# One fused kernel on one core: a one-column Exp behind each Gelu batch, layer 0 in order k, q, v, own rings for passed-on images, three PSUM buffers for the experts' first layer

## The chip, the cores and the metric

The kernel runs on one core of one Trainium2 chip. The metric is the device time of one execution in microseconds (us), as the median of several runs. The engines are named as the profile names them: PE (TensorE, matmuls; PEld its weight loads), ACT (ScalarE), DVE (VectorE), POOL (GpSimd) and SP (SyncE, which here only issues DMAs). SBUF is the on-chip memory with 128 partitions, PSUM the memory that PE writes, in eight banks of 512 float32 columns.

## What is computed

Four residual layers on x of shape (8, 384, 32, 32), all in float32, each layer of the form x + f(groupnorm(x)). Cut to what matters here:

```python
# layer 0: depthwise 3x3, batch norm, Gelu, 1x1 projection for q, k and v; attention; projection; batch norm
y = gelu(bn(depthwise3x3(x)))                 # for each of q, k, v, with own weights
q, k, v = (einsum('oc,bchw->bohw', pw, y) for ...)   # 8 heads of 48
attn = softmax(einsum('bhcn,bhcm->bhnm', q, k) * 48 ** -0.5)
out = bn(einsum('oc,bchw->bohw', w_out, einsum('bhnm,bhcm->bhcn', attn, v)))
# layer 1: 4 experts of one hidden layer (384 -> 384 -> 384, relu), weighted by a top-2 gate
hdn = relu(einsum('bchw,edc->ebdhw', x, w1) + b1)
out = einsum('ebohw,ebhw->bohw', einsum('ebdhw,eod->ebohw', hdn, w2) + b2, coef)
# layer 2: depthwise 7x7 with reflected edges, plus bias
# layer 3: three branches of depthwise convolutions (1, 3, 5) and small MLPs, fused by a gate, projected
```

## The kernel before

An image is N = 1024 pixels, the 384 channels are NC = 3 tiles of 128 partitions, there are B = 8 images. The program runs in stages, told apart in the profile by their lines: layer 0's depthwise convolution (to about 277 us), attention (to about 1745 us), the experts of layer 1 (to about 2705 us), then layers 2 and 3.

The order of instructions on PE, ACT and DVE is the order of the program text (`tc.manual_schedule`); in layer 0's convolution and from the experts on, POOL's too. The order on SP is the planner's. Each engine works in its own order and waits on semaphores for others. A tile pool gives each `tag` a ring of `bufs` buffers; a new tile of a tag waits until the readers of the tile that had its buffer are done. With `reuse_waits="tile"` dependencies are kept by tile.

**Layer 0 (L431 to L538).** `groups` runs over channel tile ct, over v = 0, 1, 2 (q, k, v) and over u = 0..3, a quarter of the output; m = n // 4 numbers the nine (ct, v) pairs. One step is 96 matmuls into one of two four-bank PSUM tiles, then `evict_slots` copies the tile to `o` on ACT (L365). While pair m runs, DVE handles pair m - 1 in `results` (L458): per image a transpose, two `bn_stats` and a store to `raw[v][b]` in DRAM. When the last channel tile of q or k has been handled, `coefs0` turns its statistics into the scale and shift of the batch norm. For image 0, q and k are loaded back to `ys0` and put through Gelu by `gelu0` while v is being convolved: all of q before the eviction of step u = 1, all of k before that of step u = 3 (L531 and L533). After the loop come the eight `results` of v and its `coefs0`.

**Attention (L561 to L913).** For each image: Gelu of q (`activate(b, 0)`), `project_k`, Gelu of v, `project_q`, then sixteen steps of scores and values. The Gelu of k for image b + 1 is done in the middle of image b (L873). At image 0 q and k come from `ys0`, and v's Gelu stands between the second and third tile of `project_q` (L843). `project` and `scores` take two-bank PSUM tiles from a ring of three (`two_banks`, L620). `scores` fills one tile by PE for each of four m and empties it by an Exp on ACT (L736). Gelu and Exp need different activation tables, and a table load (ACT_TABLE_LOAD) is placed by the compiler before an ACTIVATE whose table isn't loaded. `spread` (L634) moves q and k from PSUM to their tiles with an affine on ACT and copies on DVE (for k of image 0 all on ACT). At the end (L877 to L913) the last output projection collects three PSUM results `outs`; ACT copies each to `z`, and DVE takes moments from each. From these follow the coefficients of the next norm (`middle`, L919).

**Experts (L1087 to L1331).** For each image b and half h: twelve hidden tiles `ph` of three logical matmuls each (L1302), each emptied by a Relu on ACT into `hs` (L1306); DVE adds pairs of hidden tiles (`sums`), after k = 9 for the first three experts and at the end for the fourth; then fifteen `products` (L1213) that DVE adds to the residual `r`. In h = 1 `logits` computes the gate of the image (PSUM tiles `pl` and `pt`). In h = 0 of the next image the steps of `next_layer` stand between the Relus, at k = 0, 2, 3, 4, 5, 6: moments, group sums (`gn_ps`), coefficients and then `pass_on` for ct = 0, 1, 2. `pass_on` (L991) norms a channel tile on ACT into `xn2`, transposes it on DVE into `x2`, lets POOL copy the reflected edges and has SP store it to `x2mem` (L999). For the last image `pass_on` comes with the first matmuls of layer 2, and its first tile goes to layer 2's input directly.

Of the kernel before, what the change touches and what calls it, by code (L numbers as in the profile page):

```python
# [136 lines left out]
def conv_mixer_kernel(ctx: ExitStack, tc: tile.TileContext, a: dict, out: bass.AP):  # L137
# [11 lines left out]
    mhalf = const.tile([P, 24], FP, name="mhalf")  # L149
    nc.gpsimd.memset(mhalf, -0.5)  # L150

    one = const.tile([P, 1], FP, name="one")
    nc.gpsimd.memset(one, 1.0)
    parity = const.tile([P, 2], FP, name="parity")
# [158 lines left out]
    def affine(o, i, s, t, func=AF.Identity):  # L313
        nc.scalar.activation(o, i, func, bias=t, scale=s)  # L314
# [45 lines left out]
    def evict_slots(o, ps, at):  # L360
# [3 lines left out]
        ps = ps.rearrange("p (i e) c b h -> p (b h) i (e c)", i=2)  # L364
        nc.scalar.copy(o, ps)  # L365

    ORDERED = {mybir.EngineType.PE, mybir.EngineType.Activation, mybir.EngineType.DVE}
    ys0 = {}
    pre_pool, cxb_pool = ExitStack(), ExitStack()
    cxb = cxb_pool.enter_context(tc.tile_pool(name="cxb", bufs=1, side="right"))  # L370
    with (
# [38 lines left out]
        with tc.tile_pool(name="cps", bufs=2, space=PSUM, reuse_waits="tile") as cps:  # L410
# [17 lines left out]
                    xt0s[ct][:, :, b, 1 : 1 + H].rearrange("p c h -> p h c"), img(xn)  # L428
                )

            groups = [(ct, v, u) for ct in range(NC) for v in range(3) for u in range(4)]  # L431
            weights0 = {}

            def weights_of(n):
# [26 lines left out]
                bn_stats_of(stats[:, v * NC + ct, 2 * b : 2 * b + 2, :], y)  # L461
                nc.sync.dma_start(out=raw[v][b][:, ct, :], in_=y)

            def gelu0(v):

                for ct in range(NC):
                    i, y = v * NC + ct, ys0[v][:, ct, :]
                    affine(y, y, bn_s[:, i : i + 1], bn_t[:, i : i + 1], AF.Gelu)

            def coefs0(v):  # L470
                i = slice(v * NC, (v + 1) * NC)
# [9 lines left out]
            for n, (ct, v, u) in enumerate(groups):  # L481
                if u == 0:

                    o = co.tile([P, B, H, 32], FP, tag="o", name="o")
                w = weights0.pop(n).rearrange("p r t w -> p r (t w)")
                ps = cps.tile([P, 4, 2, B, H], FP, tag="ps", name="ps")
                for cc in range(2):
                    for k in range(3):
                        for e, d, i in product(range(2), repeat=3):
                            r = slice(64 * i, 64 * i + 64)  # L490
                            nc.tensor.matmul(  # L491
                                ps[64 * d : 64 * d + 64, 2 * i + e, cc],
                                lhsT=w[r, 12 * cc + 6 * e + 3 * d + k, :],
                                rhs=xt0s[ct][r, 16 * d + 4 * u + 2 * e + cc, :, k : k + H],
                                start=k == 0, stop=k == 2,
                            )
                spread0(n + 2)
                weights_of(n + 3)
                m = n // 4
                if n < 2:  # L500
                    for b in range(4 * n, 4 * n + 4):
                        stats2(b)
                if n == 1:
                    norm = gn_steps((mvx[:, 0], mvx[:, 1]), slot0)
                    nc.gpsimd.dma_start(out=xstmem, in_=xst)
                    nc.vector.tensor_copy(gmx, next(norm))
                if n == 2:
                    norms[1] = norms[2] = next(norm)
                for b in {3: (0, 1), 4: (2, 3), 8: (4, 5), 9: (6,), 10: (7,)}.get(n, ()):
                    prepare0(1, b)  # L510
                if m in (3, 4, 5) and u < 2:
                    for b in ((0, 1), (2,), (3, 4), (5,), (6, 7), ())[2 * (m - 3) + u]:
                        prepare0(2, b)
                if (m, u) == (5, 3):
                    cxb_pool.close()
                    pp0 = pre_pool.enter_context(
                        tc.tile_pool(name="pre0", bufs=1, side="right", reuse_waits="tile")
                    )
                    pw = pp0.tile([P, 2, NC, NC, P], FP, tag="pw", name="pw")
                    for i, k in enumerate("qk"):  # L520
                        nc.sync.dma_start(out=pw[:, i], in_=a[f"pw_{k}"])
                if m > 0:
                    for b in ((0,), (1, 2), (3, 4), (5, 6, 7))[u]:
                        results(*last, b, last_o)
                if ct == NC - 1 and v > 0 and u == 1:
                    y0 = pp0.tile([P, NC, N], FP, tag=f"y{v - 1}", name="y0")
                    nc.sync.dma_start(out=y0, in_=raw[v - 1][0])
                    ys0[v - 1] = y0
                if ct == NC - 1 and v > 0 and u == 3:
                    coefs0(v - 1)  # L530
                if m == 8 and u in (1, 3):  # L531
                    gelu0(u // 2)
                evict_slots(o, ps, u)  # L533
                if u == 3:
                    last, last_o = (ct, v), o
            for b in range(B):
                results(*last, b, last_o)
            coefs0(2)  # L538


    zraw = [dram.tile([P, NC, N], FP, tag=f"z{b}", name=f"z{b}") for b in range(B)]
# [9 lines left out]
    def layers(again, early, xst, pre_pool, pp0, pw):  # L551
# [9 lines left out]
        def attention(shifted):  # L561
# [3 lines left out]
            with tc.tile_pool(name="aw", reuse_waits="tile", bufs=1) as aw, tc.tile_pool(  # L565
# [45 lines left out]
                        nc.sync.dma_start(out=y, in_=raw[v][b])  # L611
                        ys[b].append(y)

                def activate(b, v):
                    for ct in range(NC):
                        i = v * NC + ct
                        y = ys[b][v][:, ct, :]
                        affine(y, y, bn_s[:, i : i + 1], bn_t[:, i : i + 1], AF.Gelu)

                def two_banks():  # L620
                    return scp.tile([P, 2, HF], FP, tag="sc", name="sc")
# [212 lines left out]
                for i, t in enumerate(todo):  # L834
                    b, j = t[0], i % per_b
                    if j == 0:
                        begun = b == 0 and not shifted
                        if not begun:
                            activate(b, 0)
                        project_k(b)  # L840
                        if not begun:
                            activate(b, 2)
                        project_q(b, (lambda: activate(0, 2)) if begun else None)  # L843
                        if shifted:
                            shift(b)
                    complete = None
# [23 lines left out]
                        project_out(b - 1, 1)  # L870
                    if j == per_b // 2 + 3:
                        if b + 1 < B:
                            activate(b + 1, 1)  # L873
                        project_out(b, 0)


# [7 lines left out]
                        for oc in ocs:  # L884
                            project_tile(outs[oc], att3 if t == NC else att[:, t, :], oc, t, w_last)

                outs = two_banks()
                outs = [outs[:, 0, :], outs[:, 1, :]]
                project_tiles((NC, 0), range(2))
                av_last = attend(*last, keep=True)  # L890
                outs.append(two_banks()[:, 0, :])
# [98 lines left out]

        def pass_on(r, b, ct, s, t, pool):  # L991

            xn2 = pool.tile([P, 32 * HP], FP, tag="xn2", name="xn2")[:, :N]
            affine(xn2, r[:, ct, :], s[:, ct : ct + 1], t[:, ct : ct + 1])
            if ct == 0 and b == B - 1 and xts:
                return transpose_in(xts[0][:, b], xn2)
            x = pool.tile([P, 32 * HP], FP, tag="xn2", name="x2")
            transpose_in(x.rearrange("p (c h) -> p c h", h=HP), xn2)
            nc.sync.dma_start(out=x2mem[b][ct], in_=x)  # L999

# [86 lines left out]
        def experts():  # L1087
# [166 lines left out]
            def next_layer(b):  # L1254
# [7 lines left out]
                for i, (cts, co) in enumerate(zip(parts, cos)):  # L1262
# [1 line left out]
                        keep_residual(r, b)  # L1264
                    moments2(r, b, cts, mv, dq)
                    yield
                    ps = eh.tile([P, NC, 2, 1], FP, tag=("sm", "pl")[i], name="gn_ps")
                    over_groups(ps, dq, co)
                    yield
                    norm2(ps, b, co, st)  # L1270
# [3 lines left out]
                        yield  # L1274

            def logits(b):
                pl = eh.tile([P, QF], FP, tag="pl", name="pl")
                for ct in range(NC):
                    for g in range(4):
                        nc.tensor.matmul(  # L1280
# [15 lines left out]
            for b, h in product(range(B), range(2)):  # L1296
                hs = ew.tile([P, NC, E, HF], FP, tag="hs", name="hs")
                gating = logits(b)
                for k, (e, dc) in enumerate(TODO):
                    ph = eh.tile([P, HF], FP, tag="h", name="ph", bufs=2)  # L1300
                    for ct in range(NC):
                        nc.tensor.matmul(  # L1302
                            ph, lhsT=w1[:, e, ct, dc * P : (dc + 1) * P], rhs=xns[b, h][:, ct, :],
# [1078 lines left out]
```

## Time and profile before

| What | us |
|---|---|
| median of 3 runs (lowest, highest) | 3211.94 (3209.06, 3213.28) |
| the profiled execution | 3207.34 |
| its span, from first to last instruction | 3205.5 |
| PE busy | 3030.8 |
| DVE busy | 1692.7 |
| ACT busy | 1186.8 |
| POOL busy | 262.7 |
| PE busy in 40 to 277 (of 237.0) | 202.1 |
| PE busy in 277 to 340 (of 63.0) | 52.5 |
| PE busy in 1716 to 1760 (of 44.0) | 30.7 |
| PE busy in 2560 to 3205 (of 645.0) | 575.2 |

"Busy" is the time in which an engine works on an instruction; time in which it only waits is not in it. A window view gives the same for a stretch of time. A wait view names who waited, for whom, how long in total, how often and how long at most. A timeline line gives start, duration, engine, line, operation, what is written and read, and in brackets the idle time of the engine before it with what ended it. What ended a wait is inferred, and where the engine named had long been done, it was another.

### The profile page before, as it was taken

The numbers are of one execution on the slowest core, as the hardware profiler recorded it, in microseconds if no ns is written. First come the engines' busy times: TensorE is split into PE (matmuls) and PEld (weight loads), VectorE is DVE, ScalarE is ACT, GpSimd is POOL, SyncE is SP. The second block draws the span as 40 slices with busy tenths as digits, with TensorE's granted clock in tenths as the row PEclk, the third lists the DMA queues.
The fourth block names the chain that finished last, engine by engine and source line by source line (L and its number), as shares of the span: only waits on it lengthen the run. The fifth ranks groups of instructions, "written<-read, shape, count | busy, mean of one in ns | idle before, by whom it ended". The sixth has DMA issues, their size and how long they took to land.

```text
span 3205.5 us, 42222 instructions
## 1 busy us (share of the span) xinstructions
PE 3030.8 (95%) x17740; PEld 1601.8 (50%) x17740; DVE 1692.7 (53%) x2570; ACT 1186.8 (37%) x1341; POOL 262.7 (8%) x415
## 2 busy tenths in 40 slices
PE   4988999999999999999998999999999999886999
PEld 3774334343433334343433566566566666655543
DVE  6998344444444444444445464564554554457174
ACT  3654453535444353535442221211212212446520
POOL 2432000000000000000001100000000000111400
PEclk9999999999999999999998999999999999988999
DMA  6787111011101111011004021121121113876765
GB/s 220 273 282 268 39 42 62 23 62 42 59 25 59 42 42 62 23 62 43 10 25 161 21 63 40 63 63 40 63 63 40 50 44 109 325 238 227 240 226 187
DMA packets 89089, 322.84 MB, mean 101 GB/s; under 512 B 13608, under 2 KB 16000, under 8 KB 84664
## 3 DMA queue, kind: packets, MB, share of 16 engines
q1 hardware_dynamic: 64936, 251.71, 23.0%
q10 hardware_dynamic: 13776, 35.82, 3.6%
q0 software_dynamic: 10176, 32.51, 3.0%
q8 instruction: 141, 2.31, 0.3%
q14 instruction: 60, 0.49, 0.0%
HBM read 211.66 MB, written 111.68 MB: 101 GB/s over the span
## 4 chain that ended last, share of the span: by engine, by line
PE 74%; DVE 13%; DMA 6%; issue 4%; ACT 2%; POOL 1%; SPq 0%; ACTq 0%; DVEq 0%; POOLq 0%
PE av L748 14%; PE sc L729 14%; PE p L1213 11%; PE ph L1302 11%; PE sc L627 7%; PE sc L682 4%; PE sc L804 4%; DVE stats L212 3%; DVE y L460 2%; DVE hs_sum L1206 2%; DMA x<-x 1%; PE ps L1779 1%; PE po L2193 1%; PE po L2196 1%; PE po L2204 1%
## 5 line engine op out<-in xcount | busy, mean ns | idle before, releaser
L736 ACT ACTIVATE e<-sc 128x1024 f32<-128x1024 f32 x512 | 483.1, 1029 | 544.3 <-PE sc L729 544.0
L1302 PE MATMUL ph<-xn,w 128*128 128x512 f32 x1152 | 506.3, 596 | 11.2 <-ACT hs L1306 8.2
L729 PE MATMUL sc<-qT,kT 64*128 64x512 f32 x2048 | 477.6, 603 | 10.4 <-ACT e L736 10.4
L748 PE MATMUL av<-e,vT 128*64 128x512 f32 x2048 | 467.7, 598 | 0.0
L1306 ACT ACTIVATE hs<-ph,b 128x512 f32<-128x512 f32 x192 | 131.2, 687 | 706.0 <-PE ph L1302 705.6
L1302 PEld LDWEIGHTS ph<-xn,w 128*128 128x128 f32 x1152 | 217.2, 191 | 276.0 <-issue 255.9
L729 PEld LDWEIGHTS sc<-qT,kT 64*128 64x128 f32 x2048 | 185.7, 186 | 297.4 <-issue 228.9
L748 PEld LDWEIGHTS av<-e,vT 128*64 128x64 f32 x2048 | 135.5, 136 | 316.4 <-issue 316.4
L627 PE MATMUL sc<-y,pw 128*128 128x512 f32 x576 | 251.8, 598 | 5.2 <-ACT y L314 5.2
L491 PE MATMUL ps<-xt,wx 64*64 64x256 f32 x3456 | 199.0, 389 | 38.5 <-DVE xt L427 20.1
L764 DVE LOAD_MASK_SELECT sm<-av x64 | 0.9, 14 | 424.1 <-PE av L748 424.1
L1227 DVE TENSOR_TENSOR r<-r,p 128x256 f32<-128x256 f32 x416 | 157.2, 417 | 126.9 <-PE p L1213 126.1
L766 DVE RECIPROCAL inv<-sm 128x512 f32<-128x512 f32 x64 | 214.6, 3353 | 2.2
L491 PEld LDWEIGHTS ps<-xt,wx 64*64 64x64 f32 x3456 | 157.6, 138 | 78.9 <-issue 34.0
L627 PEld LDWEIGHTS sc<-y,pw 128*128 128x128 f32 x576 | 109.7, 192 | 146.9 <-issue 138.4
L1061 PE MATMUL ps<-xt,wx 64*64 64x256 f32 (+1 forms) x2912 | 158.1, 375 | 22.4 <-ACT wx L1535 13.2
L1213 PE MATMUL p<-hs_sum,wsum 128*128 128x256 f32 x768 | 173.6, 379 | 0.0
L1213 PEld LDWEIGHTS p<-hs_sum,wsum 128*128 128x128 f32 x768 | 145.9, 190 | 19.8
L1206 DVE TENSOR_TENSOR hs_sum<-hs,hs_sum 128x768 f32<-128x768 f32 (+1 forms) x192 | 147.0, 780 | 4.9
L1061 PEld LDWEIGHTS ps<-xt,wx 64*64 64x64 f32 x2912 | 111.0, 138 | 67.8 <-ACT wx L1535 15.5
L365 ACT COPY o<-ps 128x2048 f32<-128x2048 f32 x56 | 103.9, 1856 | 79.0 <-PE ps L491 48.2
L682 PE MATMUL sc<-pw_v,y 128*128 128x384 f32 x384 | 127.8, 493 | 5.3 <-ACT y L314 5.3
(319 smaller groups left out, 3250.9 us busy)
## 6 DMA issues: line engine op xcount, KB each, us to landing
raw<-y SPq DMA_DIRECT2D x72, 512.0 KB
y<-raw SPq DMA_DIRECT2D x24, 1536.0 KB
x<-x SPq DMA_DIRECT2D x23, 608.0 KB
xt<-x SPq DMA_DIRECT2D x23, 608.0 KB
w<-in_w ACTq DMA_DIRECT2D x36, 384.0 KB
xn<-in_x SPq DMA_DIRECT2D x24, 512.0 KB
x<-in_x SPq DMA_DIRECT2D x16, 768.0 KB
z<-z POOLq DMA_DIRECT2D x16, 768.0 KB, 4.3
```

The source lines that it names most:

```text
L491: nc.tensor.matmul(ps[64 * d : 64 * d + 64, 2 * i + e, cc], lhsT=w[r, 12 * cc + 6 * e + 3 * d + k, :], rhs=xt0s[ct][r, 16 * d + 4 * u + 2 ...
L627: nc.tensor.matmul(ps[:, h, :], lhsT=w[:, ct, pair, :], rhs=y[:, ct, h * HF : (h + 1) * HF], start=ct == 0, stop=ct == NC - 1,)
L682: nc.tensor.matmul(ps[:, m, :C], lhsT=y[:, ct, (m0 + m) * P : (m0 + m + 1) * P], rhs=pw_v[:, ct, :], start=ct == 0, stop=ct == NC - 1,)
L729: nc.tensor.matmul(sc[:, s, :], lhsT=kTs[b][r, pair, m * P : (m + 1) * P], rhs=qTs[b][r, pair, h * HF : (h + 1) * HF], start=True, stop=True,)
L736: nc.scalar.activation(e, sc, AF.Exp, scale=1.0 if shifted else HD**-0.5)
L748: nc.tensor.matmul(av[64 * s : 64 * s + 64, :], lhsT=vTs[0][:, m, c0 : c0 + 64], rhs=e[:, s, :], start=m == 0, stop=m == N // P - 1,)
L766: nc.vector.reciprocal(inv, sm)
L1061: nc.tensor.matmul(ps[64 * d : 64 * d + 64, 2 * i + e, c % 2, images], lhsT=w[r, d * K7 + k, :], rhs=by_slot(xts[ct])[r, 16 * d + column(c ...
L1206: nc.vector.tensor_add(rows_of(o, hs, s), rows_of(i, hs, s), rows_of(j, hs, s))
L1213: nc.tensor.matmul(ps[:, :QF], lhsT=block(w)[:, e], rhs=rows_of(x, hs, e), start=e == 0, stop=e == E - 1,)
L1227: nc.vector.tensor_tensor(out=o, in0=o, in1=ps[:, :QF], op=op)
L1302: nc.tensor.matmul(ph, lhsT=w1[:, e, ct, dc * P : (dc + 1) * P], rhs=xns[b, h][:, ct, :], start=ct == 0, stop=ct == NC - 1,)
```

## The change

Five edits:

- `activate` gets a flag: with it a one-column Exp into the tile `warm` follows the three Gelus. It is set for v of every image and for k of image b + 1.
- Layer 0 works in the order k, q, v (`VORDER`). The Gelus of k for image 0 come one at a time behind the evictions of u = 0, 1, 2 of v's last channel tile, those of q behind the last eviction.
- The last projection's first two results get a two-bank tile each, and not one between them.
- `pass_on` has a ring of one for `xn2` and a ring of two for `x2`, and not one ring of two for both.
- In the experts' PSUM pool `pl` and the last image's second `gn_ps` share the tag `sm`, and `ph` has three buffers and not two.

```diff
+    warm = const.tile([P, 1], FP, name="warm")
...
+    VORDER = (1, 0, 2)
...
-            groups = [(ct, v, u) for ct in range(NC) for v in range(3) for u in range(4)]
+            groups = [(ct, v, u) for ct in range(NC) for v in VORDER for u in range(4)]
...
-            def gelu0(v):
-
-                for ct in range(NC):
-                    i, y = v * NC + ct, ys0[v][:, ct, :]
-                    affine(y, y, bn_s[:, i : i + 1], bn_t[:, i : i + 1], AF.Gelu)
+            def gelu0(v, ct):
+                i, y = v * NC + ct, ys0[v][:, ct, :]
+                affine(y, y, bn_s[:, i : i + 1], bn_t[:, i : i + 1], AF.Gelu)
...
-                if ct == NC - 1 and v > 0 and u == 1:
-                    y0 = pp0.tile([P, NC, N], FP, tag=f"y{v - 1}", name="y0")
-                    nc.sync.dma_start(out=y0, in_=raw[v - 1][0])
-                    ys0[v - 1] = y0
-                if ct == NC - 1 and v > 0 and u == 3:
-                    coefs0(v - 1)
-                if m == 8 and u in (1, 3):
-                    gelu0(u // 2)
+                before = VORDER[m % 3 - 1]
+                if ct == NC - 1 and m % 3 and u == 1:
+                    y0 = pp0.tile([P, NC, N], FP, tag=f"y{before}", name="y0")
+                    nc.sync.dma_start(out=y0, in_=raw[before][0])
+                    ys0[before] = y0
+                if ct == NC - 1 and m % 3 and u == 3:
+                    coefs0(before)
                 evict_slots(o, ps, u)
+                if m == 8 and u < 3:
+                    gelu0(VORDER[0], u)
                 if u == 3:
                     last, last_o = (ct, v), o
+            for c in range(NC):
+                gelu0(VORDER[1], c)
             for b in range(B):
                 results(*last, b, last_o)
-            coefs0(2)
+            coefs0(VORDER[2])
...
-                def activate(b, v):
+                def activate(b, v, exp=False):
                     for ct in range(NC):
                         i = v * NC + ct
                         y = ys[b][v][:, ct, :]
                         affine(y, y, bn_s[:, i : i + 1], bn_t[:, i : i + 1], AF.Gelu)
+                    if exp:
+                        nc.scalar.activation(warm, one, AF.Exp)
...
                         if not begun:
-                            activate(b, 2)
-                        project_q(b, (lambda: activate(0, 2)) if begun else None)
+                            activate(b, 2, True)
+                        project_q(b, (lambda: activate(0, 2, True)) if begun else None)
...
                         if b + 1 < B:
-                            activate(b + 1, 1)
+                            activate(b + 1, 1, True)
                         project_out(b, 0)
...
-                outs = two_banks()
-                outs = [outs[:, 0, :], outs[:, 1, :]]
+                outs = [two_banks()[:, 0, :] for _ in range(2)]
...
-            xn2 = pool.tile([P, 32 * HP], FP, tag="xn2", name="xn2")[:, :N]
+            xn2 = pool.tile([P, N], FP, tag="xn2", name="xn2", bufs=1)
...
-            x = pool.tile([P, 32 * HP], FP, tag="xn2", name="x2")
+            x = pool.tile([P, 32 * HP], FP, tag="x2", name="x2", bufs=2)
...
-                    ps = eh.tile([P, NC, 2, 1], FP, tag=("sm", "pl")[i], name="gn_ps")
+                    ps = eh.tile([P, NC, 2, 1], FP, tag="sm", name="gn_ps")
...
-                pl = eh.tile([P, QF], FP, tag="pl", name="pl")
+                pl = eh.tile([P, QF], FP, tag="sm", name="pl")
...
-                    ph = eh.tile([P, HF], FP, tag="h", name="ph", bufs=2)
+                    ph = eh.tile([P, HF], FP, tag="h", name="ph", bufs=3)
```

## The prediction

> **What bounds the kernel now.** I read five views in this order: the page's busy table, the windows by stage, the waits on TensorE, the timeline around each kind of wait, and last the table of groups for durations. The page:
>
> ```profile
> PE 3030.8 (95%) x17740; PEld 1601.8 (50%) x17740; DVE 1692.7 (53%) x2570; ACT 1186.8 (37%) x1341; POOL 262.7 (8%) x415
> ```
>
> TensorE is the bound, so only its idle time (about 175 us of 3205.5), and stretches where it runs at a lower clock, can be won. By stage, the columns being the stretch, its length, the busy time of each engine, the granted clock and the DMA share:
>
> ```profile
> 420.00:1716.00 1296.00, 1285.57 (x4816) 498.73 (x4812) 609.07 (x743) 589.70 (x596) 33.14 (x57) 1.00 0.13 46
> 1760.00:2560.00 800.00, 789.63 (x2826) 499.95 (x2825) 424.80 (x808) 165.08 (x231) 36.47 (x54) 1.00 0.17 52
> ```
>
> Attention (420 to 1716) leaves TensorE 10.4 us idle, the experts (1760 to 2560) another 10.4. The list of waits (who for whom: total us, times, longest) says for what:
>
> ```profile
> DVE x L973 <- DMA x<-x: 59.0, 15, 5.8
> ...
> PE sc L729 <- ACT e L736: 10.4, 14, 0.7
> ...
> PE ph L1302 <- ACT hs L1306: 8.2, 7, 1.8
> ...
> PE p L1213 <- DVE r L1229: 4.3, 7, 0.7
> ```
>
> The three TensorE waits explain those 20.8 us and a little of the last image. The first line is a VectorE wait that I trace to two of them below.
>
> [...] the load starts 17 ns after the Exp before it. [...] TensorE, writing the second bank of a two-bank tile, waits for ScalarE's read of the first[...]. [...] after 5.2 us idle the 72 matmuls of L627 take 33.6 us at image 0 against 31.1 us at later images.
>
> **Part 1, the one-column Exp (L617, L842, L873).** In attention each switch from Gelu to Exp puts the load in front of the first real Exp, and it waits there for that Exp's scores:
>
> ```profile
> 494.32 2.85 PE L729 MATMUL sc<-qT,kT 64*128 64x512 f32 x12
> ...
> 495.55 1.28 ACT L736 ACT_TABLE_LOAD   x1 [3.58 <-PE sc L729]
> ...
> 497.92 1.13 PE L729 MATMUL sc<-qT,kT 64*128 64x512 f32 x4 [0.74 <-ACT e L736]
> ```
>
> TensorE fills three score buffers, and the fourth waits 0.745 us for the first Exp, late by 1.28 us. Behind the Gelus the load falls into idle time of ScalarE (6.5 us before the load at 430.97, 3.6 us here). The Exp then ends 1.28 us earlier, 0.54 us before the fourth score needs it: the gap goes whole. 14 gaps x 0.745 = **10.4 us**. Cost: 1.28 us of load, moved, plus a new ACTIVATE on one column[...] (nearest row: a copy of six columns, 166 ns). Behind it stand, at the second switch of an image, the qT evictions: the first has 0.74 us of slack (idle before 480.55) and slips some 0.8 us; its buffer is taken again only at 494.3, so nothing on TensorE moves. Without that cover each switch would cost at most 0.8 us, 5.6 us over seven images. At image 0 the load already lay in idle time: nothing.
>
> **Part 2, layer 0 in order k, q, v, Gelu behind evictions (L430, L464, L525 to L538).**
>
> ```profile
> 281.33 3.50 ACT L314 ACTIVATE y<-y,bn_t,bn_s 128x1024 f32<-128x1024 f32 x3 [9.41 <-DVE bn_t L329]
> ```
>
> ```profile
> 286.62 1.25 DVE L460 STREAM_TRANSPOSE y<-o 128x1024 f32<-128x1024 f32 x1 [5.32 <-ACT o L365]
> ```
>
> The last eviction (284.74) stands behind three Gelus that wait for coefficients which VectorE finishes at 281.30. TensorE's convolution ended at 277.4, so the eviction could run by 279.3, and VectorE could go straight on from 281.3. It loses 5.32 us there. In the new order the k Gelus lie at u = 0, 1, 2 behind evictions; the eviction at 268.32 moves before its Gelu to about 264.7, and TensorE's 2.28 us gap at 270.31 goes too. The q Gelus run at 281.3 to 284.8, while TensorE projects k (15.6 us) without waiting. The kT evictions then start at 284.8, a little after the first is ready; three score buffers hold that. What is late next is v: its results (8 x 2.46 us) and coefficients (3.2 us) end at 304.3 instead of 309.6; then SyncE, in order, issues pw_v (which waits for those coefficients), w_out and the load of y, which lands 9.7 us after its issue; the Gelu before project_v follows. All of this shifts by 5.3 us, and TensorE, done with q earlier, waits longer before project_v (about 11 us instead of 5.3). So **5.3 us** and not the sum of TensorE's gaps. Below: SyncE's order is the planner's; a 1.5 MB load of the next y now falls among the results, and the like of it at 239 cost VectorE 1.5 us, so 2 us is the low end (0 if the loads order badly). Above: 6 us.
>
> **Part 3, separate tiles for the last projection (L887).**
>
> ```profile
> 1735.46 0.70 DVE L813 BATCH_NORM_STATS2 zst<-sc 128x6 f32<-128x512 f32 x1 [1.75 <-ACT z L899]
> ```
>
> VectorE was free at 1733.71 and the first output complete at 1733.0; it waited for the second bank's copy. With its own tile it starts at 1733.75, and the others (1.12 us of matmul each, no 0.68 us gap) are ready in time. The chain moments, group sums, POOL power, xn, first ph moves by **1.7 us** (0.5 to 1.8). The ring's third buffer is free: its Exp ends at 1717.4, the first use is at 1719.6.
>
> **Part 4, own rings, and three buffers for ph (L991 to L999, L1267, L1277, L1300).**
>
> ```profile
> 1890.81 1.98 DVE L973 STREAM_TRANSPOSE x<-xn 128x1024 f32<-128x1024 f32 x1 [3.58 <-DMA x<-x]
> ...
> 1892.82 1.24 ACT L314 ACTIVATE xn<-r,st 128x1024 f32<-128x1024 f32 x1 [3.58 <-DVE x L973]
> ...
> 1894.69 0.30 PEld L1302 LDWEIGHTS ph<-xn,w 128*128 128x128 f32 x2 [1.86 <-ACT hs L1306]
> 1894.69 1.55 PE L1302 MATMUL ph<-xn,w 128*128 128x512 f32 x3 [1.03 <-ACT hs L1306]
> ```
>
> With xn2 and x2 alternating in a ring of two, x2 in effect has one buffer: the second transpose waits for the first's store, ScalarE waits with the third xn2 in front of its Relu, TensorE with ph. Two x2 buffers remove both DMA waits; the first store (issued 1887.8, landed 1890.8) is away before the third transpose wants its buffer (1891.8). xn2 keeps its one buffer in effect, so its wait of 0.6 us stays. The third ph buffer treats the same 1.0 to 1.8 us, which counts once: 1.03 + 1.07 + 1.08 + 1.07 + 1.06 + 1.07 + 1.77 = **8.15 us**. VectorE leaves the third transpose at about 1893.9 instead of 1898.7, so the sums start with the Relu that feeds them, 6.8 us before the products as they do in the halves without pass-on, and the waits of p on r go as well: **4.3 us** (0 if another lag remains). The shared sm buffer costs nothing: each user (pl, pt, gn_ps) starts many us after the last reader, or needs that reader's data anyway. If the cover failed, a logits group of 1.5 us once an image, 12 us.
>
> The last image has the same wait on the way into layer 2:
>
> ```profile
> 2727.66 2.01 DVE L973 STREAM_TRANSPOSE x<-xn 128x1024 f32<-128x1024 f32 x1 [5.83 <-DMA x<-x]
> ```
>
> Without it the third transpose runs at 2723.2. The first eviction of layer 2 (2733.63, put down to projb, in fact when the store issued at 2730.5 had landed), the weights behind it and the SyncE loads come some 4.5 us earlier. TensorE's gap of 2.50 us at 2736.67 goes, and of the 1.26 us at 2747.37 the most. Afterwards TensorE, ScalarE and the loads pace each other, so the shift should carry: **3.5 us** (0 if the next load takes it back; 4.6 at most).
>
> **Sum.** 10.4 + 5.3 + 1.7 + 8.15 + 4.3 + 3.5 = 33.3 us. The profiled execution took 3207.3 us (span 3205.5), giving 3174.0. The median shown is 4.6 us above it (3211.94), so I forecast 3178.6, rounded to **3179**. Low ends (10.4 - 5.6, 2, 0.5, 8.15, 0, 0) give 15.5 us; high ends 35.4.
>
> **Rivals.** (a) The tails take their shares back: layer 0 behind its loads, layer 2 behind its weights, p still behind r. For it: both tails move 200 to 300 GB/s. Against: they are ordered by issue and not by rate. 10.4 + 1.7 + 8.15 = 20.3 us, **3192**. (b) The load doesn't move, being placed again at the real Exp: 22.9 us remain, **3189**. Against: one set serves both, and Identity in between runs under either set now. (c) Slower: TensorE, without its pauses, is granted less clock. Place: 2075 us of matmul in the two windows; price 20.8 us for each 1%; it decides from 1.6% (33.3 / 20.8), and at 3% gives about **3241**. For it: lower clocks occur (0.82 from 1716 to 1751). Against: they stand beside idle, and both dense windows show 1.00. (d) More: gaps in layer 2 and 3 close as loads come earlier, **3166**.
>
> **How the numbers follow.** Chances: forecast 0.72 (own range 3171 to 3187), (a) 0.14, (b) 0.05, (c) 0.04, (d) 0.05. The range 3168 to 3192 takes in the forecast, most of (d), (b) and the better half of (a). About 0.2% (6.4 us) is what a measurement can tell from no change; within it lie only the far ends of (a) and a small (c): 0.03. Faster 0.94, slower 0.03.
>
> **What would show it.** Loads right behind Gelu and no TensorE wait on e; VectorE transposing v's results at 281, project_v near 316; no wait of x on its own stores and none of ph or p; the first Relu of the experts 1.7 us sooner relative to the end of attention. A wait of ph on pl, a clock below 1.00 in the two windows, or layer 2 no shorter would prove the step in question wrong.

## The result, and the profile after

The changed kernel takes **3171.07 us** (median of 4 runs, 3169.33 to 3182.1) against 3210.5 us for the kernel before in the same session: a ratio of **0.9884, 95% interval 0.986 to 0.9908**. The profiled execution took 3172.27 us, its span is 3170.5 us; before it was 3207.34 and 3205.5 us. So the two traces that are compared here differ by 35.0 us, the medians by 39.4.

The line of busy times of the page after, and two rows of the windows by stage (stretch, its length, busy time and count of PE, PEld, DVE, ACT and POOL, granted clock, DMA share, GB/s), attention first and then the experts:

```profile
PE 3023.9 (95%) x17740; PEld 1605.6 (51%) x17740; DVE 1694.7 (53%) x2570; ACT 1190.1 (38%) x1356; POOL 253.9 (8%) x415
```

```profile
416.00:1696.00 1280.00, 1280.00 (x4808) 499.93 (x4806) 607.19 (x743) 589.92 (x608) 33.13 (x57) 1.00 0.14 47
1740.00:2524.00 784.00, 784.00 (x2818) 500.55 (x2817) 423.72 (x805) 164.31 (x229) 28.73 (x54) 1.00 0.18 53
```

In both dense stretches TensorE now has no idle time at all, still at full clock. The reader should also see that its listed busy time fell by 6.9 us (3030.8 to 3023.9) although it does the same 17740 matmuls; this comes back below. The list of waits after (who for whom: total us, times, longest) has lost the three TensorE waits that were shown of before, and VectorE's wait for its own stores (its 59.0 us in front of `x` are now a wait for ScalarE, and the same figure is chance):

```profile
DVE x L977 <- ACT xn L315: 59.0, 23, 5.4
...
PE ps L1065 <- ACT wx L1539: 11.8, 5, 3.8
...
PE sc L687 <- ACT y L315: 10.9, 1, 10.9
...
PE ps L1065 <- ACT o L366: 9.5, 1, 9.5
```

Of what is left, three lines are shown: one wait for image 0's v (L687) and two of layer 2 (L1065) on ScalarE. The timeline after, at the switch that the prediction showed (start, length, engine, line):

```profile
475.01 1.28 ACT L623 ACT_TABLE_LOAD   x1
476.30 0.20 ACT L623 ACTIVATE warm<-one 128x1 f32<-128x1 f32 x1
...
489.50 3.71 PE L734 MATMUL sc<-qT,kT 64*128 64x512 f32 x16
```

The load lies right behind the Gelus, 15 us ahead of the first score, and the 16 matmuls of the scores run as one piece of 3.71 us; before they were two, of 12 and 4 (2.85 and 1.13 us), with a gap of 0.74 us between.

Five landmarks of each trace carry the comparison. All are starts of TensorE instructions in us from the start of the span: the first matmul of image 0's v, the last matmul of attention's last projection, the first ph of the experts, the first matmul of layer 2, and the end of the span. The last column is the median time of that kernel's runs.

| kernel | v | attention ends | first ph | layer 2 | end | median |
|---|---|---|---|---|---|---|
| before | 321.52 | 1735.07 | 1751.12 | 2705.44 | 3205.48 | 3210.5 |
| after | 317.33 | 1716.11 | 1731.23 | 2669.07 | 3170.45 | 3171.07 |
| e1_no_exp | 315.43 | 1728.56 | 1743.67 | 2681.30 | 3185.90 | 3187.72 |
| e2_stall_plus | 317.60 | 1738.79 | 1753.91 | 2691.84 | 3190.80 | 3192.64 |
| e3_layer0_back | 322.21 | 1721.47 | 1736.58 | 2674.67 | 3177.04 | 3175.64 |
| e4_one_ring | 319.19 | 1718.50 | 1733.62 | 2687.32 | 3188.36 | 3186.51 |
| e5_two_ph | 315.78 | 1715.39 | 1730.51 | 2668.77 | 3171.78 | 3172.73 |
| e6_small_loads_late | 316.57 | 1714.84 | 1729.96 | 2667.53 | 3168.45 | 3174.02 |
| e7_exp_alone | 323.86 | 1723.10 | 1739.14 | 2695.22 | 3194.59 | 3194.42 |
| e8_after_again | 313.16 | 1712.69 | 1727.81 | 2666.03 | 3164.95 | 3171.27 |
| e9_fetch_pool | 319.69 | 1718.85 | 1733.98 | 2672.00 | 3164.43 | 3164.63 |
| e10_weights_by_sp | 316.79 | 1716.34 | 1731.47 | 2669.69 | 3155.40 | 3157.3 |
| e11_order_only | 323.57 | 1723.18 | 1738.31 | 2676.56 | 3175.40 | 3177.75 |
| e12_all | 319.47 | 1718.25 | 1733.37 | 2671.22 | 3165.22 | 3156.36 |

Between the two kernels the stretches differ by 4.2 us up to v, 15.7 from there to the first ph, 16.5 from there to layer 2, and -1.3 in the rest: 35.0 us. The forecast had 5.3, 12.1, 12.45 and 3.5 us there, so the parts were tried by themselves.

Only the tiles of the last projection (part 3) had no kernel of their own, but the traces separate them. From the first matmul of the last av group, at 1723.27 us before and 1705.26 us after, to the first ph it takes 27.84 us in both kernels with the shared tile (before and e7) and 25.96 to 25.98 us in all twelve with separate tiles: **1.87 us**. (With the 14.2 us of the Exp, below, that makes 16.1; the two traces show 15.7, and this stretch scatters by as much.) TensorE's wait of 0.68 us for ScalarE's copy of the first result (before, at 1733.68 us) is gone with the shared tile: its last six matmuls there run as one piece of 2.84 us. VectorE's first moments, which the prediction showed waiting 1.75 us for ScalarE's copy of the other bank, now start without a gap:

```profile
1715.64 0.70 DVE L818 BATCH_NORM_STATS2 zst<-sc 128x6 f32<-128x512 f32 x1
```

### The profile page after: what moved, and what is told of

Its sections match the earlier page's. It is cut to its first block, busy times and chain, and to the rows that moved or that the text cites. A ratio compares the mean times of both kernels' runs of the same rounds, so it can differ in the third digit from the quotient of the medians.

```text
span 3170.5 us, 42235 instructions
## 1 busy us (share of the span) xinstructions
PE 3023.9 (95%) x17740; PEld 1605.6 (51%) x17740; DVE 1694.7 (53%) x2570; ACT 1190.1 (38%) x1356; POOL 253.9 (8%) x415
## 4 chain that ended last, share of the span: by engine, by line
PE 82%; DVE 8%; DMA 6%; issue 2%; ACT 1%; POOL 1%; SPq 0%; ACTq 0%; POOLq 0%; DVEq 0%
PE ph L1306 16%; PE sc L734 15%; PE av L753 14%; PE p L1217 13%; PE sc L632 7%; PE sc L687 4%; PE sc L809 4%; DMA w<-in_w 3%; DVE stats L213 2%; DVE y L462 2%; PE ps L1783 2%; PE po L2197 1%; PE po L2200 1%; PE po L2208 1%; DVE xt L429 1%
## 5 line engine op out<-in xcount | busy, mean ns | idle before, releaser
L1065 PE MATMUL ps<-xt,wx 64*64 64x256 f32 (+1 forms) x2912 | 159.1, 377 | 22.6 <-ACT wx L1539 11.8
L1065 PEld LDWEIGHTS ps<-xt,wx 64*64 64x64 f32 x2912 | 109.1, 138 | 70.8 <-ACT wx L1539 14.1
L687 PE MATMUL sc<-pw_v,y 128*128 128x384 f32 x384 | 128.2, 495 | 10.9 <-ACT y L315 10.9
```

The source lines that it names most:

```text
L687: nc.tensor.matmul(ps[:, m, :C], lhsT=y[:, ct, (m0 + m) * P : (m0 + m + 1) * P], rhs=pw_v[:, ct, :], start=ct == 0, stop=ct == NC - 1,)
L1065: nc.tensor.matmul(ps[64 * d : 64 * d + 64, 2 * i + e, c % 2, images], lhsT=w[r, d * K7 + k, :], rhs=by_slot(xts[ct])[r, 16 * d + column(c ...
```

## The experiments

### How far a landmark scatters

The changed kernel once more, unchanged.

> The changed kernel as it is, once more, for how much each landmark scatters from one profiled execution to the next: project_v at 317.3 us, project_v to the end of attention 1398.8, from there to layer 2 953.0, from there to the end 501.4. If all come again within 0.3 us, differences of 1 to 3 us between kernels in layer 0 and in layers 2 and 3 belong to the edits; if project_v or the last stretch scatters by 2 us or more, they do not.

The middle stretches came again to 0.75 us or better (1399.53, 15.12 and 938.22 us). The outer ones did not: v started at 313.16 instead of 317.33 and the last stretch, from layer 2 to the end, took 498.92 instead of 501.38 us. Over all ten runs with the new layer 0 (e12, which asks for v's load earlier, among them), v starts between 313.2 and 319.7 us, mean 317.1. So a difference of 1 to 3 us in layer 0, or in layers 2 and 3, between two single traces is no finding; means over several kernels are used there.

### The one-column Exp, and what a stall of TensorE costs

Taken out of the changed kernel:

```diff
                         affine(y, y, bn_s[:, i : i + 1], bn_t[:, i : i + 1], AF.Gelu)
-                    if exp:
-                        nc.scalar.activation(warm, one, AF.Exp)
```

> The changed kernel without the one-column Exp; all else stays. Theory 1 (a stall costs more than the idle time that is listed for it): the end of attention moves later by 14 x 1.02 = 14.3 us, each score group behind a table load goes from 3.63 back to 4.65 us, and the listed idle time there is only 0.745 us. Rival (the listed idle time is the whole cost, and the other 3.8 us came from something else in attention): 14 x 0.745 = 10.4 us later, and the groups go to 4.38 us. Time about 3185 to 3187 under theory 1, about 3182 under the rival.

From v to the end of attention it takes 1413.13 us instead of 1398.78, so 14.35 us more; the median is 3187.72 us instead of 3171.07. The sum of all score groups on TensorE, each from its first matmul to the next group of another kind, went from 465.0 to 479.2 us, 14.2 for 14 groups: a whole group takes 3.63 us, a broken one 4.65. Yet the listed wait is again 14 times 0.745 us, 10.4 in all. Timeline of this kernel at the same switch:

```profile
488.76 2.85 PE L732 MATMUL sc<-qT,kT 64*128 64x512 f32 x12
492.35 1.13 PE L732 MATMUL sc<-qT,kT 64*128 64x512 f32 x4 [0.75 <-ACT e L739]
```

Read the lengths: 2.85 + 1.13 = 3.98 us of busy time for 16 matmuls that are 3.71 us in one piece. The stall costs its gap of 0.745 us **plus the 0.27 us** by which the two pieces are longer than one. How 1.02 us divide into gap and length is the view's, which models the ends of matmuls; the sum stands on starts alone. What the 0.27 us consist of, no run here shows. Theory 1 holds. The next kernel asks whether the 0.27 us is per stall or in proportion to it. It has no one-column Exp, and makes each of the 14 stalls longer by an Identity in front of the late Exp (`switched` is filled where the flag of `activate` is given, left out here):

```diff
                         e = ay.tile([P, 2, HF], FP, tag="e", name="e", bufs=2 * GM)
+                        if switched:
+                            switched.pop()
+                            affine(e[:, 0, :], sc[:, 0, :], 1.0, 0.0)
```

> As the kernel without the one-column Exp, and with an Identity over one bank (128x512, from PSUM) ahead of the first Exp of each of the 14 score groups behind a table load, so that the stall of TensorE grows by one ScalarE instruction of about 0.56 us. Theory 1 with a fixed surcharge per stall: the listed idle time goes from 0.745 to about 1.30 us and each such group from 4.65 to about 5.21 us, so attention ends 14 x 0.56 = 7.8 us after that of the kernel without the Exp. Rival (the surcharge is in proportion to the idle time, 1.02 / 0.745 = 1.37): groups of 5.41 us, 10.7 us later. Rival (no surcharge): groups of 4.38 + 0.56.

Its timeline:

```profile
490.78 2.85 PE L734 MATMUL sc<-qT,kT 64*128 64x512 f32 x12
...
492.02 0.60 ACT L315 ACTIVATE e<-sc 128x512 f32<-128x512 f32 x1 [3.60 <-PE sc L734]
492.63 1.28 ACT L744 ACT_TABLE_LOAD   x1
...
495.00 1.13 PE L734 MATMUL sc<-qT,kT 64*128 64x512 f32 x4 [1.38 <-ACT e L744]
```

The Identity took 0.60 us and the listed gap grew by 0.632 (1.377 against 0.745). The score groups together grew by 8.8 us, from 479.2 to 488.0, which is 0.63 each; with a surcharge in proportion it would have been 0.87. The two pieces are still 2.85 and 1.13. So in these groups the surcharge is **fixed, one per stall**, over the two lengths tried. Then the Exp in the kernel before, by itself:

> The kernel before with the one-column Exp alone. Theory 1: 14 score groups of 3.63 instead of 4.65 us, project_v to the end of attention 1398.8 instead of 1413.5 us, about 14.3 us off the whole, so about 0.9955 of the kernel before. Rival (the gain needs the other parts): less than 12 us.

Score groups 465.0 us in sum, v to the end of attention 1399.24 instead of 1413.55: 14.3 us, with none of the other parts. The ratio to before is 0.9955 (0.9941 to 0.9968). The part stands alone.

### Layer 0: the order or the place of the Gelus

All of layer 0 as before, in the changed kernel:

```diff
-    VORDER = (1, 0, 2)
+    VORDER = (0, 1, 2)
...
+                if m == 8 and u in (1, 3):
+                    for c in range(NC):
+                        gelu0(u // 2, c)
                 evict_slots(o, ps, u)
-                if m == 8 and u < 3:
-                    gelu0(VORDER[0], u)
```

(and no Gelus behind the loop).

> The changed kernel with layer 0 as it was: order q, k, v and both Gelu batches ahead of evictions in the last group. Theory: project_v starts 4.2 us later (321.5 instead of 317.3), 3.8 us are still there at the first table load of image 1, and all later landmarks move by that amount. Rival (the layer-0 part is hidden by the load of image 0's v, which sets the start of project_v): under 1 us.

v starts at 322.21 us, 4.9 later, and what follows is moved by about that. Against the means it is clearer: with the old place of the Gelus (before, e3, e7) v starts at 322.5 on average, with the new layer 0 at 317.1, so the part is worth **5.4 us**. Then the new order with the Gelus ahead of evictions:

```diff
-                if m == 8 and u < 3:
-                    gelu0(VORDER[0], u)
...
+                if m == 8 and u in (1, 3):
+                    for c in range(NC):
+                        gelu0(VORDER[u // 2], c)
                 evict_slots(o, ps, u)
```

> The changed kernel with layer 0 in order k, q, v, but both Gelu batches ahead of evictions as before. Theory (project_v waits for image 0's v, so only the evictions, through VectorE's results and the coefficients, set its start): project_v at 322.5 us as with the old layer 0 (321.5 to 323.9 in three kernels), so none of the gain is the order's. Rival (k first lets project_k start sooner, and that counts): 319 us or less, against 313.2 to 319.2 (mean 316.4) in seven kernels with the whole change.

v starts at 323.57 us, outside the 313.2 to 319.7 us of the new layer 0, and the median is 3177.75 us. The order alone gains nothing. The old order with the Gelus behind evictions was not run. Timeline of this kernel where the results of v begin, and under it that of the changed kernel:

```profile
284.23 3.50 ACT L315 ACTIVATE y<-y,bn_t,bn_s 128x1024 f32<-128x1024 f32 x3 [9.54 <-DVE bn_t L330]
287.64 1.84 ACT L366 COPY o<-ps 128x2048 f32<-128x2048 f32 x1
...
289.52 1.25 DVE L462 STREAM_TRANSPOSE y<-o 128x1024 f32<-128x1024 f32 x1 [5.32 <-ACT o L366]
```

```profile
275.38 1.87 ACT L366 COPY o<-ps 128x2048 f32<-128x2048 f32 x1 [2.17 <-PE ps L491]
...
282.32 0.16 DVE L330 TENSOR_TENSOR bn_t<-bn_gb,bn_t 128x3 f32<-128x3 f32 x1
282.40 1.25 DVE L462 STREAM_TRANSPOSE y<-o 128x1024 f32<-128x1024 f32 x1
```

With the Gelus ahead, the last eviction waits for coefficients and three Gelus, and VectorE stands 5.32 us, exactly as before. With the Gelus behind, the eviction is long done and VectorE goes on without a gap. TensorE's own order in between can be of little account, since it waits 10.9 us for v anyway.

### The experts: which ring did what

xn2 and x2 in one ring of two again, three buffers for ph kept:

```diff
-            xn2 = pool.tile([P, N], FP, tag="xn2", name="xn2", bufs=1)
+            xn2 = pool.tile([P, 32 * HP], FP, tag="xn2", name="xn2")[:, :N]
...
-            x = pool.tile([P, 32 * HP], FP, tag="x2", name="x2", bufs=2)
+            x = pool.tile([P, 32 * HP], FP, tag="xn2", name="x2")
```

> The changed kernel with xn2 and x2 again in one ring of two buffers; three PSUM buffers of layer 1 stay. Theory: the wait of the products' first matmuls comes back (0.93 us per image, 0.66 of it listed, 7 images, and 0.57 at the last one: about 7 us) while the expert hidden groups stay at 23.26 us; layer 2 starts about 7 us later, and of that up to 3 us are made good in layer 2, where the changed kernel now waits for a weight load. Rival (the one ring holds up the whole of VectorE's queue, and the hidden groups of layer 1 stall as well): about 16 us. Rival (three PSUM buffers alone take both waits): 0.

From the first ph to layer 2 it takes 953.70 us instead of 937.84: **15.9 us**, nearly all that the stretch had gained (16.5). The theory fell: it expected 7. The first rival's number came, but not in its way, since no ph stalls. The list of waits of this kernel:

```profile
DVE x L977 <- DMA x<-x: 56.9, 15, 4.3
...
PE p L1217 <- DVE r L1233: 13.7, 7, 2.1
```

and its timeline in the first image with pass-on:

```profile
1879.22 1.98 DVE L977 STREAM_TRANSPOSE x<-xn 128x1024 f32<-128x1024 f32 x1 [3.94 <-DMA x<-x]
...
1892.75 1.99 PE L1217 MATMUL p<-hs,wsum 128*128 128x256 f32 x8 [1.98 <-DVE r L1233]
```

The third ph buffer did take the wait of ph away. But VectorE, held by the stores, still comes late to its sums and to r, and TensorE, there sooner by what it had saved, waits for r by so much longer: 2.0 us in place of 1.0 for ph and 0.7 for p, or, counted from start to start, about 2.3 us in place of 1.33 and 0.93. So VectorE's chain should set the pace, and the ph wait be time that TensorE would have spent at p. That gave a new theory and the opposite kernel: own rings, two buffers for ph (and the old PSUM rings for the group sums and the gate, left out here).

```diff
-                    ph = eh.tile([P, HF], FP, tag="h", name="ph", bufs=3)
+                    ph = eh.tile([P, HF], FP, tag="h", name="ph", bufs=2)
```

> The changed kernel with two PSUM buffers for layer 1 and the group sums' and gate's own PSUM rings as before; the images' own rings stay. Theory 2 (formed after the run with the one ring: both waits of TensorE came from the one ring, whose stores hold up VectorE and, behind xn2, ScalarE; the third PSUM buffer only shifts the wait from ph to p): no wait of ph comes back, layer 2 starts 953 us after the end of attention as in the changed kernel, within 1 us. Rival (each part takes its own wait, as predicted): the hidden groups of layer 1 go back from 23.26 to 24.59 us in six images and to 25.30 in the last, 10.0 us in all.

No wait of ph on a Relu is listed, and the first ph to layer 2 takes 938.26 us against 937.84. The median, 3172.73 us, is the changed kernel's. The own rings did all of it; the third PSUM buffer does nothing beside them.

### Layer 2: where its share went

At the start of layer 2 the forecast 3.5 us came and went. The listed gap before L1065 (2.50 us, now 0.42) and the one of any_at (1.26 us) are gone, and then a stall of 1.32 us has become one of 3.84. TensorE before, at that stall:

```profile
2747.49 12.51 PE L1061 MATMUL ps<-xt,wx 64*64 64x256 f32 x224
2761.33 30.94 PE L1061 MATMUL ps<-xt,wx 64*64 64x256 f32 x560 [1.32 <-ACT wx L1535]
```

The changed kernel at the same place:

```profile
2707.66 12.51 PE L1065 MATMUL ps<-xt,wx 64*64 64x256 f32 x224
...
2711.03 1.23 ACT L1539 ACTIVATE wx<-xn,parity 128x448 f32<-128x448 f32 x2 [2.08 <-PE ps L1065]
...
2720.26 0.90 SPq L335 DMA_DIRECT2D fb<-in_fb  x2
...
2722.28 0.33 ACTq L1518 DMA_DIRECT2D xn<-in_w  x1
2722.74 1.23 ACT L1539 ACTIVATE wx<-w,parity 128x448 f32<-128x448 f32 x2 [10.48 <-DMA fb<-in_fb]
...
2724.02 2.60 PE L1065 MATMUL ps<-xt,wx 64*64 64x256 f32 x26 [3.84 <-ACT wx L1539]
```

Counted from the first matmul of layer 2 (2705.44 and 2669.07 us), the 224 matmuls start after 42.05 us before and 38.59 us after, so 3.5 us sooner; the matmuls behind the stall start after 55.89 and 54.95 us, only 0.9 us sooner.

ScalarE does nothing for 10.5 us, although the weights that it spreads next are there (landed by 2704.7 us). In its queue stands an issue of a weight load (L1518), and that waits for a small load of SyncE (fb, landed at 2722.2) whose completion semaphore, the same one (110 in the trace), it is to use. SyncE came to fb only at 2720.26 us, 8 us after ScalarE had stopped, so most of the wait is for SyncE's queue and little for the transfer. The kernel before stood at the same issue, behind another of these loads (mw, semaphore 109 for both, landed at 2759.5). Counted again from the first matmul of layer 2, ScalarE passed it after 54.16 us before (2759.60) and after 53.21 us now (2722.28): SyncE's loads came only 0.95 us sooner, and that is what is left of TensorE's 3.5 us. The first test moved the 13 loads of layer 3's constants, fb among them, from the first tile of layer 2 into the second:

```diff
+                    if ct == 1 and c == 4:
+                        load3()
                     if ct == 0 and c == 4:
-                        load3()
```

> The changed kernel with the 13 small loads of layer 3 asked for 12 groups later, in the second tile of layer 2 instead of the first. Theory: ScalarE's weight load at 2722 us stood behind one of them for its semaphore; the wait of 10.5 us in front of wx goes, and with it TensorE's stall of 3.84 us; layer 2 to the end takes 497 to 499 us instead of 501.4. Rival (the weights themselves are late, since the images' loads are ahead of them in the DMA engines): the stall stays within 1 us or shows up at the next weight block, and the time does not change.

The last stretch took 500.92 us; TensorE's stalls in the first 100 us of layer 2 are 2.3, 3.0 and 4.3 us instead of 0.4, 3.8 and 3.3. The edit didn't do what it was meant to: SyncE's order is the planner's, and in the trace it issues these loads from 2711.8 to 2724.4 us, near where they were (2708.1 to 2722.2), only behind two loads of r. So this run doesn't tell the theory from the rival. Two others do. First, the eight loads of y for layer 3, in front of which ScalarE stands 9.2 us later on, issued by GpSimd:

```diff
             for half in range(2):
-                nc.sync.dma_start(
+                nc.gpsimd.dma_start(
                     out=y[64 * half : 64 * half + 64, :], in_=y2mem[HB * half + q][1, 0:64, :]
```

> The changed kernel with layer 3's 8 first loads of y (y2mem, second channel tile) issued by GpSimd instead of SyncE, so that ScalarE's weight load at 2837.7 us no longer waits for the semaphore of one of them. Theory 3 (an issuing engine stands still until the semaphore of its transfer is free; here 9.2 us of ScalarE, 8.7 to 9.5 us of TensorE): that stall falls below 3 us and the time by 4 to 8 us, to about 3164 to 3168; what is late next is the first transposed image (4.1 us now). Rival (the DMA engines, busy 0.85 of that stretch, set the pace; the stall only moves on): no change within 2 us.

The waits of this kernel: the stall that was 9.5 us is 2.3 (last line), and the one behind fb, which this edit leaves alone, stays.

```profile
PE ps L1065 <- ACT wx L1539: 13.2, 5, 4.5
...
PE ps L1065 <- ACT o L366: 2.3, 1, 2.3
```

The last stretch takes 492.43 us and the median is 3164.63, 6.4 us below the changed kernel. The intervals of the two just overlap (0.984 to 0.9871 against 0.986 to 0.9908); of the eight executions of the changed kernel (3166.8 to 3182.1) two are below the slowest of these four (3162.3 to 3167.8). Then all weight loads issued by SyncE:

```diff
-        def load_weights(queue=nc.scalar):
+        def load_weights(queue=nc.sync):
```

> The changed kernel with all of layer 2's and 3's weight loads issued by SyncE, so that no load stands in ScalarE's queue. Theory 3: ScalarE's waits of 10.5 and 9.2 us ahead of wx go, TensorE's stalls of 3.8 and 9.5 us shrink, and layer 2 to the end falls from 501.4 (scatter 498.9 to 504.6 over the kernels so far) to below 495. Rival (in the first 90 us of layer 2 the DMA engines are 0.85 to 0.98 busy and set the pace): the first 90 us stay, and weights queued behind images come later than now: 0 to 10 us slower.

The last stretch takes **485.71 us** and the median is **3157.3 us** (ratio to before 0.9839, 0.9825 to 0.9852). Two windows of layer 2, of the changed kernel and then of this one (columns as above), and under them TensorE in this kernel, where the stall of 3.84 us had been:

```profile
2700.00:2730.00 30.00, 26.16 (x446) 17.49 (x442) 1.87 (x8) 13.91 (x20) 2.46 (x7) 0.94 0.85 318
2730.00:2760.00 30.00, 26.75 (x492) 17.50 (x488) 21.37 (x32) 12.47 (x18) 4.21 (x12) 0.98 0.98 365
```

```profile
2700.00:2730.00 30.00, 28.55 (x522) 19.84 (x518) 5.05 (x19) 15.32 (x22) 4.60 (x12) 1.00 0.85 310
2730.00:2760.00 30.00, 30.00 (x556) 20.71 (x552) 23.98 (x35) 16.84 (x23) 3.42 (x10) 1.00 0.97 371
```

```profile
2709.23 61.65 PE L1065 MATMUL ps<-xt,wx 64*64 64x256 f32 x1120
```

The DMA share and the rate are nearly the same (0.85 and 0.98 against 0.85 and 0.97), and TensorE does 1078 matmuls instead of 938. Nor do the weights come sooner: the two loads that ScalarE issued at 2705.87 and 2722.28 us are issued by SyncE at 2710.24 and 2724.32 us. So the busy DMA engines do not set the pace there, which was the rival's reason; ScalarE's queue, standing at an issue, does. The choice of the issuing engine is worth 14 us of the whole here (medians 3171.07 and 3157.3), and not for the time of issuing (0.33 us): an engine that computes stood still with it, for 10.5 us in the case shown.

The last kernel puts both together, and asks for image 0's v ahead of w_out at the start of attention.

> The kernel with the weight loads issued by SyncE, and with layer 3's first loads of y issued by GpSimd, and image 0's v asked for ahead of w_out at the start of attention. Theory: image 0's v (landed at 315.96 us behind pw_v and w_out) comes about 2 us sooner, so TensorE's wait of 10.9 us ahead of project_v falls to about 9; the 2.7 us left at the eviction in layer 3's first conversion fall to 0 to 2. 2 to 5 us below the 3157.3 us of SyncE's loads alone. Rival (the DMA engines set both places): within 2 us of it.

3156.36 us (ratio to before 0.9833, 0.982 to 0.9847), within 2 us of the one before, so the rival's number. The wait at the eviction fell from 2.7 to 0.8 us. v landed 8.3 us behind its issue instead of 9.7, and TensorE waits 10.3 us ahead of it instead of 10.9: a gain that the scatter of layer 0 hides. The profiled execution of this kernel was the slowest of its five (3167.0, the others 3153.3 to 3157.5), so the end of its trace is not compared. Its last stretch, 494.0 us, also warns that one trace can be some 8 us off there; the medians carry the gain from SyncE's loads. Either of the last two kernels is faster than both kernels of the change by more than their intervals.

## Why the prediction was right, and where its terms were off

3179 us was forecast and 3171.07 came, inside the range and at the lower edge of the forecast's own (3171 to 3187); the sum was 33.3 us against 35.0 in the traces. The mechanisms of the first three parts were right, and that of the fourth in the main. That the sum comes so close is luck: parts 1 and 4 were forecast some 8 us too small together, and the beginning of layer 2 some 4.5 us too large.

- **Part 1, 10.4 us forecast, 14.3 measured.** The mechanism is right: the load (15 times 1283 ns ahead of an Exp, before as after) moves behind the Gelus, the first Exp ends in time, the gap goes whole, and the switch, with a one-column Exp of 0.20 us (203 ns on average), costs nothing. The mis-sized term is "14 gaps x 0.745". A stall costs 1.02 us, its gap and the 0.27 us by which a broken group is longer than a whole one. The lines for it stood in the prediction: 2.85 and 1.13 us for 12 and 4 matmuls, of which only the length of a whole group was missing.
- **Part 2, 5.3 us forecast, 4.2 in the two traces, 5.4 over the means.** Right, and for the reason given, VectorE's 5.32 us. The wait ahead of v grew to 10.92 us ("about 11"). What was not separated is the order from the place of the Gelus: the order alone gave nothing.
- **Part 3, 1.7 us forecast, 1.87 measured.** Right, a little above its high end of 1.8.
- **Part 4, 8.15 + 4.3 us forecast, 16.5 measured.** Here the sum was too small for the same reason as in part 1: six images gained 1.33 us at ph where the listed gap was about 1.06, and about 0.93 at p for 0.66 (in the last image 2.04 and 0.57). The assignment was half right. The prediction said that the third ph buffer "treats the same" wait as the rings and counted it once, which held. What it did not say is that the buffer alone would have earned next to nothing, since the saved time is spent at p: with it and the one ring, e4's stretch is 953.70 us against 954.32 before.
- **The beginning of layer 2, 3.5 us forecast, about -1 measured.** Over seven kernels with the own rings and ScalarE's weight loads (e6 left out, whose edit lies in this stretch) the last stretch takes 501.2 us on average, over three with the one ring (before, e4, e7) 500.2. The seven scatter from 498.8 to 504.6, so this is nothing gained rather than a loss. The early gain is there in the trace, and of 3.5 us 0.9 are left behind the next stall. "Layer 2 no shorter" was the prediction's own sign of an error. The step that failed is "Afterwards TensorE, ScalarE and the loads pace each other, so the shift should carry". They pace each other through ScalarE's queue: ScalarE stands at an issue until the load of SyncE whose semaphore it needs has landed (10.5 us behind fb), and that landing came 0.95 us sooner, not 3.5. Why SyncE's loads came no sooner was not tried. For this part rival (a) was right in the outcome; its reason, the DMA engines' rate, was not. That the queue is the cause is shown for the stalls of 3.84 us (by e10) and 9.5 us (by e9); how the gain is lost in the other places of layers 2 and 3 stays open.
- **Rivals (b), (c) and (d).** The load moved, and behind it the affines of qT and the Exps run without another load (15 ahead of an Exp and 15 ahead of a Gelu in both traces); the clock is 1.00 in both dense windows; the last stretch got no shorter. So none of them came.
- **Slips without weight.** The high ends add up to 35.25 us, not 35.4, and the 72 matmuls of L627 take 31.17 us at later images, not 31.1.

## What to carry to other kernels

Price a stall of a busy TensorE by comparing the broken group with a whole one, first matmul to first matmul of what follows, and not by the listed gap: the fixed part (0.27 us in the scores here, for gaps of 0.745 and 1.377 us) counts once for each stall. Where two waits follow each other in one loop, look for what they have in common before adding them up; a buffer that removes the first may only lengthen the second, as here (953.70 us with it and the one ring, 954.32 before). Keep DMA issues that can wait for a semaphore out of the queue of an engine that computes: ScalarE stood 10.5 us at one here.

## What was not expected of the hardware

- A stall of TensorE in the scores costs 0.27 us more than its listed gap, for gaps of 0.745 and of 1.377 us alike; in the experts the difference is the same (1.33 for 1.06, 0.93 for 0.66).
- ScalarE stood 10.5 and 9.2 us at the issue of a load whose data nobody needed yet; with the same loads issued by SyncE the whole took 14 us less (medians 3157.3 and 3171.07).
- Ten executions with the new layer 0 reach image 0's v between 313.2 and 319.7 us, while attention with the Exp (1398.3 to 1399.6 us) and the experts with own rings (937.6 to 938.3) come again far more closely.
